# Selective-scan units of 32 channels by 4 states, with delta, du, B and C laid out by DMA

## The chip, the cores and the metric

One core of one Trainium2 chip runs the whole program: eight images go through two vision-Mamba layers in one launch. TensorE (PE), VectorE (DVE), ScalarE (ACT) and GpSimd (POOL) each work through their own instructions in order, and SyncE (SP) issues every DMA of this kernel. The metric is device time in microseconds of one execution. Data are float32, apart from a few bf16 tiles.

## The reference

Layer 0 maps each image of 64 by 64 tokens and 192 channels through a projection, a depthwise convolution, a two-directional SSD scan with 12 heads and 32 states, an output projection and an MLP. Layer 1 splits the channels in halves. One half goes through three convolutions; the other through layer norm, a projection to 192 channels, a depthwise convolution and a selective scan in four directions, after which the results are summed, normalised, gated and projected.

The change is in layer 1's selective scan:

```python
# per image and direction k: 192 channels, 16 states, L = 4096 tokens
x_dbl = jnp.einsum('bkdl,kcd->bkcl', xs4, x_proj_w)
dts, Bs, Cs = x_dbl[:, :, :6], x_dbl[:, :, 6:22], x_dbl[:, :, 22:]
delta = softplus(jnp.einsum('bkrl,kdr->bkdl', dts, dt_proj_w) + dt_proj_b)
A = -jnp.exp(A_logs)
def step(h, t):
    u_t, d_t, b_t, c_t = t
    h = jnp.exp(d_t[..., None] * A) * h + (d_t * u_t)[..., None] * b_t[:, :, None, :]
    return (h, jnp.einsum('bkdn,bkn->bkd', h, c_t))
```

So for every channel and state there is a recurrence along the tokens, h = dA * h + dB, with dA = exp(delta * A), dB = delta * u * B. Its results are multiplied by C and summed over the states. Here du stands for delta * u.

## The kernel before

**The scan's tiling.** `selective_scan` works in steps of LC = 1024 tokens: per image four steps forward (g = 0) and four backward (g = 1), each with two of the four directions. The 2 x 192 channels of a step are three tiles of 128 channels (t = 0, 2, 1; t = 2 holds the upper 64 channels of both directions). A unit of work is one [128, 1024] tile, whose partitions are 8 channels (UD) times 16 states (NS); a channel tile has 16 units (UN), and there are 8 x 8 x 3 x 16 = 3072 units in all.

**What a unit does.** For unit q:
- `fetch` (L1445) is a DMA that brings delta of its 8 channels from DRAM, each row repeated for 16 states, into a tile dA; it is issued 6 units ahead (AHEAD), into a ring of 7 tiles.
- `decay` (L1450) turns it into dA = exp(delta * A) on ScalarE, two units ahead and in place.
- `spread` (L1458) makes du repeated over the states in PSUM, by two matmuls of a 0/1 matrix with du in three bf16 terms that add up to the float32 value. Two PSUM tiles of two banks each are used in turn.
- `weigh` (L1473) multiplies that in PSUM by B, on VectorE.
- `scan` (L1480) is VectorE's recurrence h from dA, dB and the carry of the step before; behind it GpSimd multiplies h by C in place (L1482), all but the last column.
- `carry_on` (L1488, L1489) runs one unit later on ScalarE: it copies h's last column to the carry, and multiplies it by C.
- `gather` (L1500) runs every four units: TensorE sums four units' h over their states into a PSUM bank for each half of 512 tokens, ScalarE copies it to y (L1505), and `store` issues four DMAs (L1513).

**What feeds it.** `prepare` makes delta and du of the next channel tile: two matmuls, softplus on ScalarE, a product on GpSimd (L1409). Delta goes to DRAM (L1412); du is split into three bf16 terms by two casts on ScalarE (L1417, L1421) and two subtractions on GpSimd (L1419, L1423), goes to DRAM (L1426) and comes back as the matmuls' operand by twelve DMAs (L1434). `lay` (L1386) loads B and C, each row repeated for the 8 channels, as one tile each for a step and a direction.

**The order.** All instructions are pinned in the order in which the program writes them. The loop over q writes the scan's own pieces. In each half of a unit `Beside.half` adds pieces of the other work, as much as a credit allows: the next image's layer 0 (`conv0`, `ssd`, `mlp0`), and, for earlier images, `conv_branch`, `scan_outputs`, and the sums. So every engine's queue, SP's among them, mixes scan and other work in a fixed order. Those generators allocate their PSUM banks from a ring (`Shared.one`), of 4 banks while the scan runs; `gather` uses it too.

Of the kernel before, what the change touches and what calls it, by code (L numbers as in the profile page):

```python
# [17 lines left out]
L = HH * WW  # L18
PW = WW + 2
C = 192  # L20
# [19 lines left out]
UD = 128 // NS  # L40
UN = 128 // UD
# [34 lines left out]
class Shared:  # L76
# [5 lines left out]
    def __init__(self, tc):  # L82
        self.tc, self.nc, self.pin = tc, tc.nc, tc.keep_in_program_order
        self.k = {}
        self.singles = []
        self.side = None

# [22 lines left out]
def setup(cx, cp, dp, p0, p1):  # L110
# [141 lines left out]
    fold = cp.tile([128, UD], F32, tag="fold", name="fold")  # L252
    nc.vector.tensor_copy(fold, ident[:, 0:UD])
    for i in [32 * g + UD * v for g in range(4) for v in range(3)][1:]:
        nc.vector.tensor_add(fold, fold, ident[:, i : i + UD])
    for g in range(4):
        nc.vector.tensor_copy(
            k["spread"][32 * g : 32 * (g + 1), :].rearrange("p (n c) -> p n c", c=UD),
            bcast(fold[32 * g : 32 * (g + 1), 0:UD], 1, NS),
        )  # L260
    col = cp.tile([128, UD], F32, tag="col", name="col")
    nc.vector.tensor_copy(col, ident[:, 0:UD])
    for n in range(1, NS):
        nc.vector.tensor_add(col, col, ident[:, UD * n : UD * (n + 1)])
    k["gather"] = cp.tile([128, 32], F32, tag="gather", name="gather")
    nc.gpsimd.memset(k["gather"], 0.0)
    nc.vector.tensor_copy(k["gather"][:, 0:UD], col)
# [110 lines left out]
def conv0(cx, x):  # L378
# [3 lines left out]
    with cx.pool("cw0") as wp, cx.pool("v0", 2) as vp:  # L382
# [51 lines left out]
        def convolve(p, j):  # L434
            pss = [cx.one("ps_cv") for i in range(2)]
            yield from depthwise(cx, pss, [diag[0:64, j], diag[64:128, j]], pads[j])
            for i, ps in enumerate(pss):
                xc = xcs[p, 2 * j + i] = vp.tile([128, 512], F32, tag="xc", name="xc", bufs=7)
                pin(nc.scalar.activation(xc, ps, AF.Silu, bias=k["cb"][:, 2 * j + i : 2 * j + i + 1]))
            cx.exp_again()  # L440

        def turn(p, q):
# [26 lines left out]
            for rows, t in ((k["xrows"], xo), (k["prows"].rearrange("l k m -> l (k m)"), po)):  # L469
                at = p * R2 * WW  # L470
                dst = rows[at : at + R2 * WW].rearrange("(b q t) c -> q t b c", b=2, t=128)[q]
                pin(nc.sync.dma_start(out=dst, in_=t))
# [27 lines left out]
        for p in range(NP):  # L500
# [8 lines left out]
            for q in range(4):  # L509
                yield from turn(p, q)  # L510


def ssd(cx):
# [16 lines left out]
    with cx.pool("g0", 2) as gp, cx.pool("s0", 2) as sp:  # L530
# [72 lines left out]
        def decays(c):  # L603

            both = groups[c // GC][0]
            X = sp.tile([128, 2, NH, HP], F32, tag="X", name="X")
# [50 lines left out]
        def outputs(c):  # L657
# [19 lines left out]
            yield None  # L677
            psh = [cx.one("ps_h")[:, :INNER0] for d in range(2)]
# [7 lines left out]
            ps = pss[1].rearrange("p (h c) -> p h c", c=HP)  # L686
            pin(nc.vector.tensor_add(Hn, ps, Hn))
# [31 lines left out]
def mlp0(cx, x, x1):  # L719
# [9 lines left out]
    with cx.pool("mw0") as wp, cx.pool("m0", 2) as mp:  # L729
# [8 lines left out]
        def loads(i):  # L738
# [10 lines left out]
            def load_y(v, d):  # L749
                t = mp.tile([128, 2, INNER0], F32, tag=f"y{d}", name=f"y{d}", bufs=4 - 2 * d)  # L750
# [86 lines left out]
        def contract(i):  # L837
# [8 lines left out]
            pin(nc.sync.dma_start(out=x1[0:128, i * 2 * T : (i + 1) * 2 * T], in_=oa))  # L846
            for v, low in enumerate(lows):
                pin(nc.sync.dma_start(out=x1[128:C, (2 * i + v) * T : (2 * i + v + 1) * T], in_=ob[low]))
# [24 lines left out]
        for i in range(1, NI + 1):  # L873
# [7 lines left out]
            if i < NI:  # L881
                yield from project(i)


def conv_branch(cx, xl, short, out, side=None):

    nc, pin, k = cx.nc, cx.pin, cx.k
    with cx.pool("cw1") as wp, cx.pool("a1", 2) as ap:
# [49 lines left out]
        def second(r):  # L938
            ps = cx.one("ps_c2")[:CH]
            yield from conv(ps, pads[1][r % 2], ws[1])  # L940
            ys[r] = ap.tile([CH, 512], F32, tag="y", name="y")
# [331 lines left out]
class Beside:  # L1273
# [14 lines left out]
    def half(self):  # L1288

        self.cx.aside()  # L1290
# [13 lines left out]
    def finish(self):  # L1304

        for gen in self.stages:
            total = sum(cost or 0.0 for cost in gen)
# [4 lines left out]
def selective_scan(cx, us, ys, beside, images, start_image, tail):  # L1312
# [9 lines left out]
    AHEAD, BEHIND = 6, 2  # L1322
# [7 lines left out]
    units = [(n, i) for n in range(len(tiles)) for i in range(UN)]  # L1330
    U = len(units)
# [12 lines left out]
    with (  # L1344
# [4 lines left out]
        tc.tile_pool(name="ps1w", bufs=2, space=PSUM) as pw,  # L1349
    ):  # L1350
        u_of, rows_of, bc_of, delta_of, du_of, carries = {}, {}, {}, {}, {}, {}
        dAs, dBs, hs, late = {}, {}, {}, []
# [29 lines left out]
        def lay(m, e, i):  # L1382

            t = wp.tile([128, LC], F32, tag=f"bc{i}{e}", name=f"bc{i}{e}")
            at = NS * (2 * i + e)
            pin(nc.sync.dma_start(out=t, in_=repeated(rows_of[m][1][at : at + NS], True)))  # L1386
            bc_of.setdefault((m, e), []).append(t)

        def prepare(n):
# [8 lines left out]
            dl, du = (wp.tile([128, LC], F32, tag=v, name=v) for v in ("dl", "du"))  # L1398
# [10 lines left out]
            pin(nc.gpsimd.tensor_mul(du, dl, u_of[m][t]))  # L1409
            yield 6  # L1410
            dld = dp.tile([128, LC], F32, tag="dld", name="dld")
            pin(nc.sync.dma_start(out=dld, in_=dl))  # L1412
            delta_of[n] = dld
            yield 7

            terms = wp.tile([128, 3, LC], BF16, tag="terms", name="terms")
            pin(nc.scalar.copy(terms[:, 0, :], du))  # L1417
            yield 9
            pin(nc.gpsimd.tensor_sub(du, du, terms[:, 0, :]))  # L1419
            yield 11  # L1420
            pin(nc.scalar.copy(terms[:, 1, :], du))  # L1421
            yield 13
            pin(nc.gpsimd.tensor_sub(terms[:, 2, :], du, terms[:, 1, :]))  # L1423
            yield 17
            dud = dp.tile([3, 128, LC], BF16, tag="dud", name="dud")
            pin(nc.sync.dma_start(out=dud.rearrange("s p l -> p s l"), in_=terms))  # L1426
            yield 21

            dus = np_.tile([128, UN // 2, 512], BF16, tag="dus", name="dus")
            for half in range(2):  # L1430
# [7 lines left out]
                if half == 0:  # L1438
                    yield 23
# [299 lines left out]
```

## Time and profile before

| what | value |
|---|---|
| median of three runs | 16418.63 us (16416.5 to 16457.44) |
| span of the profiled execution | 16436.7 us |
| first scan starts, last scan starts | 902.0 us, 16192.7 us |
| mean granted TensorE clock | 0.827 |
| DMA | 3241.31 MB, 197 GB/s over the span; the queue's packets fill 78.5% of 16 engines |

DMA issues of the scan, all by SP:

| issue | count | KB each |
|---|---|---|
| dA<-dld (L1445) | 3072 | 512 |
| dud<-terms (L1426) | 192 | 768 |
| dus<-dud (L1434) | 2304 | 64 |
| bc<-bcd (L1386) | 256 | 512 |
| dld<-dl (L1412) | 192 | 512 |
| y<-y (L1513) | 3072 | 32 |

The longest waits of SP's own queue: 3764.0 us at L1445 for VectorE's scan (L1480) to free a tile of the ring, 474.6 us at L1445 for the DMA dA<-dld before it, 353.6 us at L607 (X<-xrows) for TensorE.

How to read it: a group's line has the code line, engine and operation, out<-in by the program's names, the shape, the count, then busy us and mean ns of one, then the engine's idle time just before that group and what ended most of it. The page's chain of waits is followed back from the last instruction, and its shares say on what the span was spent. Idle time of an engine that holds nothing up costs nothing.

### The profile page before, as it was taken

To read this page: it belongs to the slowest core of one execution; us is meant where nothing else is said; L and a number is where in the kernel's file an instruction comes from. 1 tells how busy PE (TensorE), PEld (TensorE's weight loads), DVE (VectorE), ACT (ScalarE), POOL (GpSimd) and SP (SyncE) were. 2 spreads that over 40 slices of the span, in tenths; PEclk is the share of its full clock that TensorE was granted. 3 is DMA by queue.
4 is the path that set the end of the run, shared out by engine and by line. 5 is a ranking of instruction groups with operands and counts; after the bars stand their busy time and mean duration, and the time that the engine had idled before them with its cause. 6 is when DMAs were issued, how large, how long until landed. Compare 5 with 4: busy or idle time off the path is not lost.

```text
span 16436.7 us, 210821 instructions
## 1 busy us (share of the span) xinstructions
PE 13372.1 (81%) x69608; PEld 4636.5 (28%) x69608; DVE 12230.0 (74%) x9264; ACT 10412.7 (63%) x20023; POOL 10527.5 (64%) x5766
## 2 busy tenths in 40 slices
PE   8977887788877897878888788777898788878876
PEld 4423322332223321333223332233322333211111
DVE  2178887886878767887678876788767886778994
ACT  4466677665775757757576575766657666655654
POOL 3158766775668656686567765677656775566773
PEclk9987888789887897878888798887988779877766
DMA  3288888788887888878888778887778877888885
GB/s 89 84 218 195 210 205 225 190 204 208 204 219 187 205 205 207 209 191 204 208 208 207 198 196 198 217 205 197 204 193 221 198 202 205 193 227 200 211 204 137
DMA packets 1602582, 3241.31 MB, mean 197 GB/s; under 512 B 390152, under 2 KB 841368, under 8 KB 1601496
## 3 DMA queue, kind: packets, MB, share of 16 engines
q1 hardware_dynamic: 1601496, 3227.83, 78.5%
q8 instruction: 559, 9.16, 0.3%
q14 instruction: 527, 4.32, 0.1%
HBM read 2548.91 MB, written 678.18 MB: 196 GB/s over the span
## 4 chain that ended last, share of the span: by engine, by line
PE 30%; DMA 16%; DVE 14%; ACT 13%; POOL 7%; issue 5%; SPq 2%; DVEq 0%; ACTq 0%; POOLq 0%
DVE h L1480 9%; DMA dA<-dld 5%; PE acc L1500 5%; DVE dB L1473 4%; PE ps_c L895 4%; PE ps_cv L343 3%; POOL h L1482 3%; ACT dA L1450 3%; PE dB L1458 2%; DMA dus<-dud 2%; PE ps_sum L1193 1%; ACT L107 1%; PE ps_m L799 1%; PE ps_y L696 1%; ACT h L830 1%
## 5 line engine op out<-in xcount | busy, mean ns | idle before, releaser
L1482 POOL TENSOR_TENSOR h<-h,bc 128x1023 f32<-128x1023 f32 x3072 | 7228.8, 2354 | 4585.2 <-DVE h L1480 3895.8
L1480 DVE TENSOR_TENSOR_SCAN h<-dA,carry,dB 128x1024 f32<-128x1024 f32 x3072 | 7200.8, 2344 | 820.7 <-ACT dA L1450 257.6
L1473 DVE TENSOR_TENSOR dB<-dB,bc 128x1024 f32<-128x1024 f32 x3072 | 3736.3, 1216 | 1827.5 <-PE dB L1458 1823.9
L1450 ACT ACTIVATE dA<-dA,neg_a 128x1024 f32<-128x1024 f32 x3072 | 3512.9, 1144 | 29.3 <-DMA dA<-dld 24.1
L1500 PE MATMUL acc<-h,gather 128*32 128x512 f32 x12288 | 2364.1, 730 | 596.5 <-ACT h L1489 329.0
L1458 PE MATMUL dB<-dus,spread 24*128 24x512 bf16 x6144 | 1370.2, 435 | 664.5 <-DVE h L1480 620.1
L1505 ACT COPY y<-acc 128x512 f32<-128x512 f32 x1536 | 884.8, 576 | 750.3 <-PE acc L1500 677.4
L895 PE MATMUL ps_c<-p,conv_w 96*96 96x512 f32 x2304 | 1287.7, 685 | 37.9 <-ACT p L915 26.9
L1488 ACT COPY carry<-h 128x1 f32<-128x1 f32 x3072 | 584.2, 190 | 856.9 <-DVE h L1480 854.4
L1458 PEld LDWEIGHTS <-spread 24*128 24x128 bf16 x6144 | 308.0, 93 | 2837.2 <-issue 1395.5
L1489 ACT ACTIVATE h<-h,bc 128x1 f32<-128x1 f32 x3072 | 905.2, 295 | 143.3 <-ACT carry L1488 1.8
L696 PE MATMUL ps_y<-X,M 64*64 64x64 f32 x12288 | 605.6, 270 | 418.6 <-issue 232.7
L624 ACT ACTIVATE M<-ps_d,ln_dt 128x64 f32<-128x64 f32 x3072 | 669.1, 335 | 314.6 <-PE ps_d L630 304.6
L343 PE MATMUL ps_cv<-pad,diag 64*64 64x512 f32 x6912 | 841.0, 605 | 7.1 <-ACT y L1505 5.1
L1500 PEld LDWEIGHTS acc<-h,gather 128*32 128x32 f32 x12288 | 311.2, 117 | 1636.3 <-issue 1040.1
L107 ACT ACT_TABLE_LOAD x577 | 740.3, 1283 | 10.0
L696 PEld LDWEIGHTS ps_y<-X,M 64*64 64x64 f32 x12288 | 548.8, 180 | 606.5 <-issue 275.5
L629 PE MATMUL ps_d<-R,after 128*128 128x384 f32 x1024 | 606.4, 685 | 31.2 <-ACT bc L618 14.6
L895 PEld LDWEIGHTS ps_c<-p,conv_w 96*96 96x96 f32 x2304 | 372.6, 180 | 785.5 <-issue 725.4
L618 ACT COPY bc<-ps_t 64x256 f32<-64x256 f32 x256 | 93.4, 365 | 716.7 <-PE ps_t L613 716.5
L373 PE MATMUL ps_h<-oa,w1a 128*128 128x256 f32 x1536 | 484.0, 438 | 76.6 <-ACT y L1505 32.2
L1370 PE MATMUL ps_xp<-u,xp 128*108 128x512 f32 x768 | 470.0, 699 | 92.5 <-DMA u<-u 76.0
(243 smaller groups left out, 18412.4 us busy)
## 6 DMA issues: line engine op xcount, KB each, us to landing
dA<-dld SPq DMA_DIRECT2D x3072, 512.0 KB
dud<-terms SPq DMA_DIRECT2D x192, 768.0 KB
dus<-dud SPq DMA_DIRECT2D x2304, 64.0 KB
bc<-bcd SPq DMA_DIRECT2D x256, 512.0 KB
y<-yrows SPq DMA_DIRECT2D x256, 384.0 KB
u<-u SPq DMA_DIRECT2D x192, 512.0 KB
dld<-dl SPq DMA_DIRECT2D x192, 512.0 KB
y<-y SPq DMA_DIRECT2D x3072, 32.0 KB
```

Source lines behind the costliest of these rows:

```text
L107: self.pin(self.nc.scalar.preload_act_table_set("natural_log_exp_and_others"))
L343: pin(nc.tensor.matmul(ps[64 * b : 64 * (b + 1)].rearrange("p (h w) -> p h w", w=WW), lhsT=diag[:, t, :], rhs=pad[64 * i : 64 * (i + 1), b ...
L696: pin(nc.tensor.matmul(psy[d][here, h * HP : (h + 1) * HP], lhsT=M[here, d, h, :], rhs=X[here, d, h, :], start=True, stop=True,))
L895: pin(nc.tensor.matmul(ps.rearrange("p (h w) -> p h w", w=WW), lhsT=w[:, t, :], rhs=pad[:, dy : dy + RB, dx : dx + WW], start=t == 0, stop ...
L1450: pin(nc.scalar.activation(dAs[q], dAs[q], AF.Exp, scale=k["neg_a"][:, steps[m][1], t, i : i + 1]))
L1458: pin(nc.tensor.matmul(dBs[q][:, half, :], lhsT=k["spread"][at : at + 3 * UD, :], rhs=du_of[n][at : at + 3 * UD, i // 2, :], start=True, s ...
L1473: pin(nc.vector.tensor_mul(dBs[q], dBs[q], of(q)[0]))
L1480: pin(nc.vector.tensor_tensor_scan(order(h, g), order(dA, g), order(dB, g), carry, ALU.mult, ALU.add))
L1482: pin(nc.gpsimd.tensor_mul(h[:, rest], h[:, rest], C_[:, rest]))
L1489: pin(nc.scalar.activation(end, end, AF.Identity, scale=C_[:, last : last + 1]))
L1500: pin(nc.tensor.matmul(ps[32 * v : 32 * (v + 1)], lhsT=k["gather"], rhs=hs[q - 3 + v][:, here], start=True, stop=True))
L1505: pin(nc.scalar.copy(y[:, here], ps))
```

## The change

A unit becomes 32 channels times 4 states (UD = 32, NU = 4). There are still 16 units to a channel tile and 3072 in all. Eight units are a group (GROUP): two blocks of 32 channels, in turn, through four groups of states.

- `fetch` now brings delta (dlr) and du (dur), each row repeated for 4 states; one tile of each serves the four units of a block. They are loaded a group ahead, in rings of four.
- `decay` reads dlr and writes dA in a ring of three.
- `spread`, its constant, the bf16 terms and dus are gone. du is made in place of u, stored as float32, and read back by `fetch`.
- `lay` loads one tile of B and one of C for every 4 states, four of each for a direction, each row repeated for 32 channels. They are issued from the scan's loop two units behind the last use of the tile that they replace.
- `weigh` multiplies B and dur, both in SBUF, into one PSUM tile of two banks. It is written right behind the scan of the unit before.
- GpSimd's product covers all 1024 columns and goes from h to a tile of its own, g (ring of four; h has a ring of three). `carry_on` comes two units later and only copies, and only where another step follows.
- `gather` runs every two units and accumulates over the four groups of states in a PSUM bank of its own, whose partitions are two halves of tokens times two blocks. So there is one y of [128, 512] in eight units, which two DMAs store.
- `Shared.later` holds a store back for some halves of a unit (y 5, xrows and prows 3, x1 2).
- Rings: xc 7 to 6, X 2 to 3, the forward y of `mlp0` 4 to 3, y of `conv_branch` to 1; the PSUM ring has 5 banks while the scan runs. In `ssd` the add to Hn stands ahead of the matmuls ps_h. In the first half of a unit `Beside.half` comes ahead of `prepare`, in the second half behind it.

```diff
-UD = 128 // NS
-UN = 128 // UD
+UD = 32
+NU = 128 // UD
+UN = 128 // UD * (NS // NU)
...
+    def later(self, halves, call):
+        self.waiting.append([halves, call])
+    def half(self):
+        for item in self.waiting:
+            item[0] -= 1
+        self.flush(0)
+    def flush(self, least=None):
+        while self.waiting and (least is None or self.waiting[0][0] <= least):
+            self.waiting.pop(0)[1]()
...
-        def lay(m, e, i):
-            t = wp.tile([128, LC], F32, tag=f"bc{i}{e}", name=f"bc{i}{e}")
-            at = NS * (2 * i + e)
-            pin(nc.sync.dma_start(out=t, in_=repeated(rows_of[m][1][at : at + NS], True)))
+        def lay(m, e, state):
+            at = NS * e + NU * state
+            for i, v in enumerate("BC"):
+                t = np_.tile([128, LC], F32, tag=v, name=v, bufs=NS // NU)
+                pin(nc.sync.dma_start(out=t, in_=repeated(rows_of[m][1][2 * NS * i + at : 2 * NS * i + at + NU], True)))
...
-            pin(nc.gpsimd.tensor_mul(du, dl, u_of[m][t]))
+            pin(nc.gpsimd.tensor_mul(du, dl, du))
...
+            pin(nc.sync.dma_start(out=dud, in_=du))
...
+        def fetch(q, which):
+            n, _, _, cg, _ = of(q)
+            tag = ("dl", "du")[which]
+            t = np_.tile([128, LC], F32, tag=tag + "r", name=tag + "r", bufs=4)
+            pin(nc.sync.dma_start(out=t, in_=repeated(delta_of[n][which][UD * cg : UD * (cg + 1)], False)))
...
+            dAs[q] = np_.tile([128, LC], F32, tag="dA", name="dA", bufs=3)
...
+        def weigh(q):
+            n, _, _, cg, _ = of(q)
+            dBs[q] = pw.tile([128, LC], F32, tag="w", name="dB")
+            pin(nc.vector.tensor_mul(dBs[q], bc(q, "B"), reps[n, cg, 1]))
+        def scan(q):
+            carry, g, _ = carry_of(q)
+            dA, dB = dAs.pop(q), dBs.pop(q)
+            h = hs[q] = np_.tile([128, LC], F32, tag="h", name="h", bufs=3)
+            pin(nc.vector.tensor_tensor_scan(order(h, g), order(dA, g), order(dB, g), carry, ALU.mult, ALU.add))
+            gs[q] = np_.tile([128, LC], F32, tag="g", name="g", bufs=4)
+            pin(nc.gpsimd.tensor_mul(gs[q], h, bc(q, "C")))
...
+        def gather(q):
+            n, m, t, cg, state = of(q)
+            image, g, s = steps[m]
+            if state == 0:
+                late.append(py.tile([128, 512], F32, tag="acc", name="acc"))
+            ps = late[-1]
+            for half in range(2):
+                for b in range(2):
+                    at = 64 * half + UD * b
+                    pin(nc.tensor.matmul(
+                        ps[at : at + UD], lhsT=k["gather"], rhs=gs[q - 1 + b][:, halves[half]],
+                        start=state == 0, stop=state == NS // NU - 1,
+                    ))
...
+                if q % 2 == 1 and q > 2:
+                    _, m0, t0, cg, state = of(q - 2)
+                    if t0 == 2 and cg == 1:
+                        lay(m0, 1, state)
+                    if t0 == 1 and cg == 3 and m0 + 1 < len(steps):
+                        lay(m0 + 1, 0, state)
...
+                ahead = q - q % GROUP + GROUP
+                if q % GROUP < 4 and ahead < U:
+                    fetch(ahead + q % 2, q % GROUP // 2)
...
                     if half == 0:
-                        if q > 0:
-                            carry_on(q - 1)
-                        if q + 1 < U:
-                            spread(q + 1)
-                        scan(q)
+                        if q > 1:
+                            carry_on(q - 2)
+                        scan(q)
+                        if q + 1 < U:
+                            weigh(q + 1)
                     elif q + 2 < U:
                         decay(q + 2)
```

## The prediction

> **What bounds the kernel now.** I read the page's totals first, then the chain of waits, the costliest groups, the stretches by stage, the waits, and a piece of the timeline.
>
> ```profile
> span 16436.7 us, 210821 instructions
> PE 13372.1 (81%) x69608; PEld 4636.5 (28%) x69608; DVE 12230.0 (74%) x9264; ACT 10412.7 (63%) x20023; POOL 10527.5 (64%) x5766
> PE 30%; DMA 16%; DVE 14%; ACT 13%; POOL 7%; issue 5%; SPq 2%; DVEq 0%; ACTq 0%; POOLq 0%
> ```
>
> No engine is full, and the chain changes hands all the time: engines that run in order wait for each other. So the question is which of these waits end, not how much work.
>
> ```profile
> L1482 POOL TENSOR_TENSOR h<-h,bc 128x1023 f32<-128x1023 f32 x3072 | 7228.8, 2354 | 4585.2 <-DVE h L1480 3895.8
> L1480 DVE TENSOR_TENSOR_SCAN h<-dA,carry,dB 128x1024 f32<-128x1024 f32 x3072 | 7200.8, 2344 | 820.7 <-ACT dA L1450 257.6
> L1473 DVE TENSOR_TENSOR dB<-dB,bc 128x1024 f32<-128x1024 f32 x3072 | 3736.3, 1216 | 1827.5 <-PE dB L1458 1823.9
> L1458 PE MATMUL dB<-dus,spread 24*128 24x512 bf16 x6144 | 1370.2, 435 | 664.5 <-DVE h L1480 620.1
> L1505 ACT COPY y<-acc 128x512 f32<-128x512 f32 x1536 | 884.8, 576 | 750.3 <-PE acc L1500 677.4
> L1488 ACT COPY carry<-h 128x1 f32<-128x1 f32 x3072 | 584.2, 190 | 856.9 <-DVE h L1480 854.4
> L1489 ACT ACTIVATE h<-h,bc 128x1 f32<-128x1 f32 x3072 | 905.2, 295 | 143.3 <-ACT carry L1488 1.8
> ```
>
> The largest wait of VectorE is in front of L1473: 1824 us until TensorE's spread (L1458) is there. That matmul is short (two of 435 ns a unit) but stands in TensorE's order behind conv and MLP matmuls.
>
> ```profile
> 889.00:16193.00 15304.00, 12457.13 (x63672) 4239.01 (x63672) 12015.65 (x8776) 9973.65 (x19078) 10265.27 (x5500) 0.82 0.82 205
> 6600.00:6900.00 300.00, 254.92 (x1868) 98.11 (x1864) 255.37 (x148) 233.54 (x440) 208.17 (x105) 0.92 0.88 223
> 6900.00:7400.00 500.00, 382.69 (x3128) 166.51 (x3128) 411.52 (x424) 283.38 (x756) 405.20 (x267) 0.74 0.76 187
> 7400.00:7800.00 400.00, 337.78 (x1513) 142.13 (x1514) 304.36 (x216) 297.29 (x488) 245.41 (x111) 0.90 0.82 204
> 7800.00:8300.00 500.00, 445.81 (x1214) 120.05 (x1212) 338.37 (x222) 293.40 (x503) 286.58 (x150) 0.86 0.79 200
> ```
>
> Columns: stretch, length, busy PE, PEld, DVE, ACT, POOL, clock, DMA share, GB/s. Scanning fills 15304 us, or 4.98 us for each of 3072 units; 889 + 244 = 1133 us lie outside. The four stages are layer 0's convolution, its SSD, its MLP, and layer 1's conv branch. VectorE leads in the first two (85% and 82%), TensorE in the last two (84% and 89%), DMA is at 0.76 to 0.88 in all.
>
> ```profile
> 15701.28 2.35 DVE L1480 TENSOR_TENSOR_SCAN h<-dA,carry,dB 128x1024 f32<-128x1024 f32 x1
> 15703.55 1.21 DVE L1473 TENSOR_TENSOR dB<-dB,bc 128x1024 f32<-128x1024 f32 x1
> 15703.77 2.35 POOL L1482 TENSOR_TENSOR h<-h,bc 128x1023 f32<-128x1023 f32 x1 [1.24 <-DVE h L1480]
> 15704.89 2.35 DVE L1480 TENSOR_TENSOR_SCAN h<-dA,carry,dB 128x1024 f32<-128x1024 f32 x1
> ```
>
> Where little else is in the way a unit takes 3.61 us (15704.89 - 15701.28), all of it VectorE's. GpSimd's product starts with VectorE's next product: the end of a scan sets off both.
>
> **The change, part by part.** Sums are against the execution of 16436.7 us; the median of the runs, 16418.6, is 18 us less.
>
> *Spread removed.* TensorE loses 6144 matmuls, 1370 us, and VectorE's wait of 1824 us has no object any more; TensorE's own waits for a free dB (1125 us before the loads, 620 us before the matmuls) go too. The gain lies between 0 (the next wait is as late) and 1824 us. Late next is ScalarE's decay, which stands behind evictions of the other layers' matmuls, so that TensorE still holds VectorE, but at two units' distance instead of one. By stage the spread costs TensorE 0.446 us a unit: 73, 85, 79 and 89 scans give 33, 38, 35 and 40 us, which bring it to 74, 69, 76 and 81%, while VectorE stays at 85, 82, 76 and 68%. The first two stages thus have little to win, the last two more. I take half: -912 us.
>
> *dB from two SBUF tiles.* Same size, same engine: 3072 x 1216 ns stays. The one row with two SBUF inputs, a 128x384 product at setup (L179), took 557 ns against 536 to 540 ns for those with a PSUM tile, so alone it costs next to nothing more (20 ns x 3072 = 61 us at most; taken as 0). What no row shows is such a product beside GpSimd: every VectorE product in the scan now has a PSUM operand. Bounds: 0, and a whole GpSimd product each time, 2354 ns x 3072 = 7231 us. In favour of the low end: GpSimd's product is as long as the scan (2354 and 2344 ns) and, if it starts behind the new product, is over when the scan is. Only GpSimd's other work can then stand in the way, 10265 - 7229 - 817 = 2219 us in 15304, 14.5% of the time, with some 0.6 us left of an operation of about 1.2 us: 0.09 us a unit. I take 0.15 us, since a product pushed back can hinder the next one: 461 us.
>
> The Trainium skill (SBUF — State Buffer, Who interferes with whom) speaks against the change here: a VectorE instruction with two SBUF inputs and a GpSimd instruction that reads SBUF exclude each other, and whichever comes second is blocked for the whole of the first. No row of this trace shows it. By that rule the sum depends on who is first after each scan: near mine if VectorE is, near the high bound if GpSimd is.
>
> *ScalarE.* Scaling the last column (L1489) goes, 905 us; the carry copy stays in 2304 of 3072 units (438 us for 584) and looks back two units, not one, so that its 854 us of waiting shrink; 384 y copies replace 1536 (221 us for 885); the two casts go (400 us). ScalarE falls by 2115 us, from 65% of the scan to 51%. It was not full, so I count nothing beyond the half above.
>
> *GpSimd.* Two subtractions per tile go (817 us); the product has one column more (2 ns). Also nothing beyond.
>
> *DMA.* Per unit dA's 512 KB becomes two such tiles per four units: 1611 MB to 805. The 2304 spread loads (151 MB) go, dud shrinks by 50 MB, B and C grow from 256 to 1024 tiles (134 to 537 MB): 604 MB less of 3228. SP issues 5376 fewer (8704 to 3328) and no longer waits in every unit for the scan to free dA (3764 us). But 128 of the 384 groups of eight units now carry eight B/C tiles and four fetches, 6.3 MB, beside 3.1 MB of other traffic: 46 us at the mean 205 GB/s, 39 us at the 242 GB/s of the fastest 100 us that I saw, against 40 us for eight units. Bounds 0 and 128 x 6 = 770 us; I take 0, as fetches are a group ahead and B and C four units, and leave it to the half given back. Each C load waits on SP for a GpSimd product two units back; behind it stand X and y loads of the other layers, which then start late.
>
> *Shorter rings, later stores, the Hn add moved up.* h falls from 7 buffers to 3 (plus 4 for the products): a scan needs the product three units back, 15 us for 2.4 us of work. xc 7 to 6 is covered by TensorE's order (its last readers come before the next writers). y 4 to 3 and the one-deep y of the conv branch are covered by loads a turn ahead; GpSimd's product of the first waits 153 us for its load now, ScalarE's write of the second 157 us for TensorE; both could double. Later stores take waits such as 156 us (SP for oa) and 108 us (for xo) off SP's order, on which nothing ends directly. The Hn add waits 230 us for GpSimd now; earlier, a whole product before each would be 256 x 2.35 = 603 us. All 0; cover gone, up to 0.9 ms together.
>
> Sum: 16437 - 912 + 461 = 15986; less 18 for the median: **15970 us**, own range 15300 to 16400.
>
> **Rivals.**
> *A, slower: GpSimd holds the product back.* Place: right behind each scan, where both start within 0.2 us. If a product meets GpSimd at any time of its work, 67% of the scan, and waits half an operation of 2354 ns, that is 0.79 us a unit, 2422 us. VectorE: 12016 busy + 2422 + (3288 - 1824) other idle + 1133 outside = 17035, or 17020. It decides from 912/3072 = 0.30 us a unit on. For it: the same start, and SSD, where GpSimd has 405 of 500 us: less 23 for the subtractions, plus 85 products of 1.22 us = 104, it is 486 us if nothing overlaps. Against: the lengths match, so the two can take turns. Chance 0.31. Its extreme, waiting out every product, gives 16437 - 912 + 7231 = 22760 us, a few per cent of that.
> *B, the wait only moves.* Decay, B/C bursts or the short rings are late exactly where the spread was. Nothing gained, with the 461 us of hindrance or without: 16420 to 16880, centre 16600. For it: DMA at 0.82 and TensorE at 81%. Against: 604 MB less. Chance 0.13.
> *C, everything is won.* 1824 us with no hindrance: 14600 to 15200. For it: 3.61 us units exist. Against: the two stages in which VectorE is already at 82 to 85%. Chance 0.10.
>
> **Numbers.** Forecast 0.46, A 0.31, B 0.13, C 0.10. Under 0.3% (49 us) a measurement cannot tell. Faster: C and nearly all of the forecast: 0.55. Same: 0.06, from the forecast's edge and B's. Slower: 0.39, from A and most of B. Range 15100 to 17100: it holds the forecast, B and the middle of A.
>
> **What would show it.** Right: L1473's successor idles little and lasts 1.2 to 1.4 us; spans on GpSimd stay near 2.35 us; VectorE is above 76% of the span. A shows as a product or a GpSimd row stretched towards 3.5 us. B shows as VectorE's idle time in front of the scan, released by dA or by B and C loads. I am wrong above all if the two engines' products cannot take turns.

## The result and the profile after

| | before | after |
|---|---|---|
| median | 16428.15 us (16416.5 to 16457.44, 4 runs) | 19802.73 us (19794.14 to 19859.58, 4 runs) |
| profiled execution's span | 16436.7 us | 19799.7 us |

The change made the kernel slower: the ratio is 1.205, 95% interval 1.203 to 1.207. The forecast was 15970 us, its range ended at 17100 us.

From the page of the changed kernel: the span, busy time by engine, the mean busy share of the 16 DMA engines in tenths over 40 slices, the DMA queue (packets, MB, share of 16 engines), the chain of waits by engine, and four groups of instructions.

```profile
span 19799.7 us, 184227 instructions
PE 13204.0 (67%) x63464; PEld 4572.6 (23%) x63464; DVE 13616.2 (69%) x9235; ACT 8490.1 (43%) x14634; POOL 12227.8 (62%) x5381
...
DMA  3234433444434444444444444444444444443333
...
q1 hardware_dynamic: 1257432, 2623.55, 40.7%
...
DVE 4%; DMA 3%; PE 1%; SPq 1%; ACT 1%; issue 0%; POOL 0%; DVEq 0%; ACTq 0%; POOLq 0%
...
L1482 POOL TENSOR_TENSOR g<-h,C 128x1024 f32<-128x1024 f32 x3072 | 9524.3, 3102 | 5431.1 <-DVE h L1480 4101.0
L1480 DVE TENSOR_TENSOR_SCAN h<-dA,carry,dB 128x1024 f32<-128x1024 f32 x3072 | 7194.5, 2342 | 3488.4 <-ACT carry L1490 1979.8
L1473 DVE TENSOR_TENSOR dB<-B,dur 128x1024 f32<-128x1024 f32 x3072 | 4979.0, 1621 | 844.1 <-DMA B<-bcd 389.9
...
L1395 PE MATMUL ps_xp<-u,xp 128*108 128x512 f32 x768 | 556.3, 836 | 1180.7 <-DMA u<-u 1178.8
```

Three things stand here. No engine is fuller than 69% although everything takes longer. The DMA engines, at 78.5% before, look idle at 40.7%, with 604 MB less to move. And yet several lines wait for a load: TensorE 1179 us for u at L1395, which was 76 us before (there the line is L1370). The wait that the change was to remove, 1824 us ahead of L1473, is down to 844, but the one ahead of the scan grew from 821 to 3488. The chain breaks off after a tenth of the span here, so it says little.

That line of TensorE before:

```profile
L1370 PE MATMUL ps_xp<-u,xp 128*108 128x512 f32 x768 | 470.0, 699 | 92.5 <-DMA u<-u 76.0
```

A low share and late loads fit together if few of the 16 engines have all the work. This is the DMA view of the changed kernel in the window from 9068 to 9100 us, in 40 slices of 0.8 us: the engines' mean busy share in tenths, and GB/s.

```profile
DMA  8699962222232222269622223843522222222222
GB/s 342 172 317 245 236 136 86 102 108 102 102 123 102 102 108 102 98 174 375 220 86 102 108 102 128 323 142 129 164 108 102 102 102 102 87 92 102 102 102 102
```

For most of the time the share is pinned at 2 tenths, which is near 4 of 16 engines, and the rate at 102 to 108 GB/s, mostly 102, or some 26 GB/s for each of four. In between other transfers reach 317 to 375 GB/s. So 512 KB over four engines take some 5.1 us (524288 bytes at 102 GB/s). The trace's DMA packets, counted over the whole span, say the same: four or five are in flight at once for 61% of it (before: 1.5%), and at least four for 91%. Before, the most frequent number was sixteen, for 32% of the span. What SP's own queue does meanwhile, from the timeline (start, duration, engine, line, operation):

```profile
9066.55 0.57 SPq L1412 DMA_DIRECT2D B<-bcd  x1
...
9068.88 5.60 SPq L1412 DMA_DIRECT2D B<-bcd  x1
9074.58 4.84 SPq L1412 DMA_DIRECT2D C<-bcd  x1
...
9082.38 5.03 SPq L857 DMA_DIRECT2D x<-oa  x1
```

An issue takes 0.57 us at first, and then about 5 us, the length of one such load, as it would if each had to wait until a load ahead of it is done. SP issues in order, so whatever stands behind it is late too, even a transfer of another stage (L857 stores layer 0's output).

The waits of the changed kernel (engine, tile, line, what it waited for: us in total, times, longest):

```profile
DVE h L1480 <- ACT carry L1490: 1979.8, 279, 38.9
...
PEld ps_xp L1395 <- DMA u<-u: 1281.7, 125, 35.8
...
DVE h L1480 <- ACT dA L1455: 1004.3, 138, 26.6
...
ACT po L472 <- DMA prows<-po: 612.0, 40, 45.2
```

These are few and long: 279 waits for the carry make 1980 us, 7.1 us each. ScalarE's carry is a copy of 0.19 us, but in ScalarE's order it stands behind evictions that wait for TensorE or for a transfer. So VectorE's idle time would largely be a late transfer seen through other engines; in experiment 1, with the loads on time, the wait for the carry falls to 453 us.

The second cost is in the durations. The scan lasts what it did (2342 ns), but dB's product has a mean of 1621 ns for 1216, and GpSimd's product 3102 for 2354. From the timeline of the changed kernel, near its end, where little else runs:

```profile
19470.79 1.23 DVE L1473 TENSOR_TENSOR dB<-B,dur 128x1024 f32<-128x1024 f32 x1
...
19470.90 3.32 POOL L1482 TENSOR_TENSOR g<-h,C 128x1024 f32<-128x1024 f32 x1 [0.41 <-DVE h L1480]
19472.15 2.35 DVE L1480 TENSOR_TENSOR_SCAN h<-dA,carry,dB 128x1024 f32<-128x1024 f32 x1
...
19478.39 2.35 POOL L1482 TENSOR_TENSOR g<-h,C 128x1024 f32<-128x1024 f32 x1 [0.43 <-DVE h L1480]
19479.49 2.33 DVE L1473 TENSOR_TENSOR dB<-B,dur 128x1024 f32<-128x1024 f32 x1 [1.25 <-DMA B<-bcd]
```

In the first unit VectorE starts 0.11 us ahead: its product takes 1.23 us and GpSimd's 3.32, 0.97 more than alone. Two units later a late B tile lets GpSimd start first: it takes 2.35 us, and VectorE's product 2.33 instead of 1.23. Whichever comes second stands still, and the profile counts that as its busy time.

So there are two suspects, and they can be undone separately. Theory D: the repeated loads run on 4 engines, since their source's outermost step is 4 long. Theory L: VectorE's product of two SBUF tiles and GpSimd's work shut each other out.

### The profile page after: what moved, and what is told of

Its sections match the earlier page's. It is cut to its first block, busy times and chain, and to the rows that moved or that the text cites. A ratio compares the mean times of both kernels' runs of the same rounds, so it can differ in the third digit from the quotient of the medians.

```text
span 19799.7 us, 184227 instructions
## 1 busy us (share of the span) xinstructions
PE 13204.0 (67%) x63464; PEld 4572.6 (23%) x63464; DVE 13616.2 (69%) x9235; ACT 8490.1 (43%) x14634; POOL 12227.8 (62%) x5381
## 3 DMA queue, kind: packets, MB, share of 16 engines
q1 hardware_dynamic: 1257432, 2623.55, 40.7%
## 5 line engine op out<-in xcount | busy, mean ns | idle before, releaser
L1482 POOL TENSOR_TENSOR g<-h,C 128x1024 f32<-128x1024 f32 x3072 | 9524.3, 3102 | 5431.1 <-DVE h L1480 4101.0
L1480 DVE TENSOR_TENSOR_SCAN h<-dA,carry,dB 128x1024 f32<-128x1024 f32 x3072 | 7194.5, 2342 | 3488.4 <-ACT carry L1490 1979.8
L1473 DVE TENSOR_TENSOR dB<-B,dur 128x1024 f32<-128x1024 f32 x3072 | 4979.0, 1621 | 844.1 <-DMA B<-bcd 389.9
L1502 PE MATMUL acc<-g,gather 128*32 128x512 f32 x12288 | 2984.9, 770 | 2064.3 <-POOL g L1482 1758.4
L1455 ACT ACTIVATE dA<-dlr,neg_a 128x1024 f32<-128x1024 f32 x3072 | 3512.0, 1155 | 1903.3 <-DVE h L1480 1647.1
L1395 PE MATMUL ps_xp<-u,xp 128*108 128x512 f32 x768 | 556.3, 836 | 1180.7 <-DMA u<-u 1178.8
L1502 PEld LDWEIGHTS acc<-g,gather 128*32 128x32 f32 x12288 | 373.9, 120 | 4060.3 <-POOL g L1482 2913.9
L674 PE MATMUL ps_s<-xw,both 64*32 64x384 f32 x2048 | 310.3, 656 | 498.3 <-POOL xw L659 464.5
L768 POOL TENSOR_TENSOR y<-y,y 128x768 f32<-128x768 f32 x128 | 256.7, 2013 | 532.7 <-DMA y<-yrows 502.5
L659 POOL TENSOR_TENSOR xw<-X,toend 128x768 f32<-128x768 f32 x256 | 381.6, 1491 | 288.6 <-DMA X<-xrows 259.4
L465 PE MATMUL ps_p<-xp,xc 64*128 64x140 f32 x3072 | 289.8, 324 | 399.3 <-ACT po L472 394.0
L1435 POOL TENSOR_TENSOR u<-dl,u 128x1024 f32<-128x1024 f32 x192 | 471.4, 2455 | 112.8 <-DMA bcd<-rows 82.0
```

The costliest lines, as they stand in the source:

```text
L1395: pin(nc.tensor.matmul(ps[:NXP], lhsT=k["xp"][:, g, t, :], rhs=u_of[m][t][:, here], start=t == 0, stop=t == 2))
L1455: pin(nc.scalar.activation(dAs[q], reps[n, cg, 0], AF.Exp, scale=k["neg_a"][:, steps[m][1], t, i : i + 1]))
L1473: pin(nc.vector.tensor_mul(dBs[q], bc(q, "B"), reps[n, cg, 1]))
L1480: pin(nc.vector.tensor_tensor_scan(order(h, g), order(dA, g), order(dB, g), carry, ALU.mult, ALU.add))
L1482: pin(nc.gpsimd.tensor_mul(gs[q], h, bc(q, "C")))
L1502: pin(nc.tensor.matmul(ps[at : at + UD], lhsT=k["gather"], rhs=gs[q - 1 + b][:, halves[half]], start=state == 0, stop=state == NS // NU - 1,))
```

## The experiments

Ratios are to the kernel before, which ran on the same chip each time (medians 16431.1, 16434.1 and 16432.3 us in the three sets).

**1. Turned.** In the changed kernel's repeated loads the outermost step of the source runs over 4: the 4 states of B and C, or the 4 repeats of delta and du. Here a channel's 4 states lie side by side, so the outermost step is 32. Bytes, tiles and instructions are the same.

```diff
-    nc.vector.tensor_copy(k["gather"], ident[:, 0:UD])
+    nc.vector.tensor_copy(k["gather"], ident[:, 0:128:NU])
...
-                pin(nc.sync.dma_start(out=t, in_=repeated(rows_of[m][1][2 * NS * i + at : 2 * NS * i + at + NU], True)))
+                pin(nc.sync.dma_start(out=t, in_=repeated(rows_of[m][1][2 * NS * i + at : 2 * NS * i + at + NU], False)))
...
-            pin(nc.sync.dma_start(out=t, in_=repeated(delta_of[n][which][UD * cg : UD * (cg + 1)], False)))
+            pin(nc.sync.dma_start(out=t, in_=repeated(delta_of[n][which][UD * cg : UD * (cg + 1)], True)))
...
-    d["a_logs"] = a.transpose(0, 1, 5, 3, 2, 4).reshape(2, 3, 128, UN)
+    d["a_logs"] = a.transpose(0, 1, 3, 5, 2, 4).reshape(2, 3, 128, UN)
```

> The changed kernel with the partitions turned: channel times 4 plus state, not state times 32 plus channel, so that the outermost step of every repeated load (dlr, dur, B, C) has 32 entries and not 4; the same bytes, issues and instructions. Theory D (a repeated load with an outermost step of 4 runs on 4 of the 16 DMA engines, at some 102 to 108 GB/s, 4.8 us for 512 KB, and SP's queue fills): the DMA share in bursts is no longer 0.22, SP's issues of 512 KB fall from up to 5 us to 0.5, time 15900 to 16900 us. Theory L (VectorE's product with two SBUF operands and GpSimd's product hinder each other, and that is the loss): nothing changes, 19300 us or more.

Measured: 16357.7 us, ratio 0.995 (0.993 to 0.997). Against the changed kernel that is 3445 us less, inside theory D's range. From its page:

```profile
span 16363.6 us, 184227 instructions
...
PE 12867.4 (79%) x63464; PEld 4473.6 (27%) x63464; DVE 13799.6 (84%) x9235; ACT 8491.2 (52%) x14634; POOL 12481.1 (76%) x5381
...
q1 hardware_dynamic: 1288152, 2623.68, 49.6%
...
L1482 POOL TENSOR_TENSOR g<-h,C 128x1024 f32<-128x1024 f32 x3072 | 9751.6, 3176 | 2718.3 <-DVE h L1480 2127.3
L1480 DVE TENSOR_TENSOR_SCAN h<-dA,carry,dB 128x1024 f32<-128x1024 f32 x3072 | 7196.5, 2343 | 971.2 <-ACT carry L1490 452.8
L1473 DVE TENSOR_TENSOR dB<-B,dur 128x1024 f32<-128x1024 f32 x3072 | 5170.4, 1683 | 207.0 <-DMA dur<-dud 101.7
```

The same 2624 MB; four or five packets are in flight for only 2% of the span, and the wait ahead of the scan is 971 us instead of 3488. Both products are still stretched, and VectorE is at 84%: with the loads on time it is the bound.

**2 and 3. One operand.** The product of the changed kernel, and of the turned one, takes one SBUF tile and a column of B; B's other columns are left out of the result.

```diff
-            pin(nc.vector.tensor_mul(dBs[q], bc(q, "B"), reps[n, cg, 1]))
+            pin(nc.vector.tensor_scalar_mul(dBs[q], reps[n, cg, 1], bc(q, "B")[:, 0:1]))
```

> The changed kernel with the product dB made from one SBUF tile: dur times the first column of B as a scalar for each partition (B's other columns are left out of the computation; all loads stay). Theory L: the product stays at 1.23 us (mean now 1.62), GpSimd's at 2.35 us (mean now 3.10), time 16000 to 17000 us. Theory D: the rows get short as well, but the 4-engine loads still bound it: 18700 to 19600 us.

> Both: partitions turned and dB from one SBUF tile (B's other columns left out of the computation). What is left is the change without either cost. Theory D plus a smaller L: 14900 to 15900 us, 400 to 1200 us below the run with turned partitions alone. Theory L alone: the same as the run with one operand.

Measured: 19508.0 us (ratio 1.187, 1.184 to 1.190) in the changed kernel, 15375.5 us (0.936, 0.934 to 0.939) in the turned one. Products of the latter, from its page's groups:

```profile
L1482 POOL TENSOR_TENSOR g<-h,C 128x1024 f32<-128x1024 f32 x3072 | 7232.2, 2355 | 4662.6 <-DVE h L1480 3672.1
...
L1473 DVE TENSOR_SCALAR dB<-dur,B 128x1024 f32<-128x1024 f32 x3072 | 3954.2, 1287 | 209.7 <-DMA dur<-dud 101.1
```

GpSimd is back at 2355 ns, and VectorE's product takes 1286 to 1290 ns, never more. So theory L is right, and its price depends on the loads: 982 us where they are on time (16358 - 15376), 295 us in the changed kernel (19803 - 19508), where VectorE waits for loads anyway. As the single-operand form is 54 ns longer than the undisturbed product (1233 ns, 166 us in all), 982 is rather a lower figure. Experiment 3 is also the change without either cost: 1056 us less than before. It changes the operation along with the operand; experiment 10 moves an operand and keeps the operation.

**4. The kernel before, turned.** The outermost step of its repeated loads is 16, and sixteen packets in flight is what its trace shows most. With a channel's 16 states side by side, delta's loads have one of 8. Nothing of the change is in this kernel.

```diff
-            pin(nc.sync.dma_start(out=dAs[q], in_=repeated(delta_of[n][UD * i : UD * (i + 1)], False)))
+            pin(nc.sync.dma_start(out=dAs[q], in_=repeated(delta_of[n][UD * i : UD * (i + 1)], True)))
```

(B and C, the constants and A's layout are turned to match.)

> The kernel before with its partitions turned the other way: channel times 16 plus state, so that the outermost step of dA's load has 8 entries and not 16, and that of B and C 8 and not 16; the same bytes and instructions, with constants to match. Theory D: those loads run on 8 engines; 1745 MB on 8 engines at 27 GB/s each is 8.1 ms, beside some 8.9 ms of each engine's other packets, so the first 8 engines are full at 17000 us: 17000 to 19000 us. Theory L, or any theory in which the order of the repeated loads does not matter: 16400 us, the same as before.

Measured: 18202.8 us, ratio 1.108 (1.105 to 1.111). Its queue and the chain of waits, from its page:

```profile
q1 hardware_dynamic: 1574872, 3227.72, 60.3%
...
DMA 37%; PE 26%; DVE 13%; ACT 9%; POOL 7%; issue 4%; SPq 3%; DVEq 0%; POOLq 0%; ACTq 0%
DMA dA<-dld 16%; DVE h L1480 8%; DVE dB L1473 4%; PE ps_cv L343 4%; PE acc L1500 3%; DMA X<-xrows 3%; DMA u<-u 3%; POOL h L1482 2%; DMA dus<-dud 2%; PE ps_c L895 2%; ACT dA L1450 2%; DMA prows<-po 2%; DMA part<-y 2%; PE dB L1458 2%; DMA xa<-in_x_dram 2%
```

The same line of the kernel before:

```profile
DVE h L1480 9%; DMA dA<-dld 5%; PE acc L1500 5%; DVE dB L1473 4%; PE ps_c L895 4%; PE ps_cv L343 3%; POOL h L1482 3%; ACT dA L1450 3%; PE dB L1458 2%; DMA dus<-dud 2%; PE ps_sum L1193 1%; ACT L107 1%; PE ps_m L799 1%; PE ps_y L696 1%; ACT h L830 1%
```

DMA's share of the chain rises from 16% to 37%, dA's loads from 5% to 16%, while the queue's busy share falls from 78.5% to 60.3%. Eight packets are in flight for 43% of the span, against 4.5% before. Order alone costs 1772 us here. That says that the order counts, and theory D's range held it, but in both kernels partitions and outermost step were changed together. The next one separates them.

**5. Split loads.** The changed kernel with its own partition order; each repeated load is four DMAs of 32 partitions, whose outermost step is 32.

```diff
-                pin(nc.sync.dma_start(out=t, in_=repeated(rows_of[m][1][2 * NS * i + at : 2 * NS * i + at + NU], True)))
+                for v4 in range(NU):
+                    row = rows_of[m][1][2 * NS * i + at + v4 : 2 * NS * i + at + v4 + 1]
+                    src = bass.AP(row.tensor, row.offset, [[0, UD], list(row.ap[1])])
+                    pin(nc.sync.dma_start(out=t[UD * v4 : UD * (v4 + 1)], in_=src))
...
-            pin(nc.sync.dma_start(out=t, in_=repeated(delta_of[n][which][UD * cg : UD * (cg + 1)], False)))
+            for v4 in range(NU):
+                pin(nc.sync.dma_start(out=t[UD * v4 : UD * (v4 + 1)], in_=delta_of[n][which][UD * cg : UD * (cg + 1)]))
```

> The changed kernel with its own order of partitions, and each repeated load (dlr, dur, B, C) issued as four DMAs of 32 partitions, so that each has an outermost step of 32; the same bytes, 10240 issues in place of 2560. Theory D (the outermost step of 4 is what counts, not the order of the partitions): 16300 to 17000 us, near the run with turned partitions, a little more for SP's 7680 extra issues of some 0.3 us. If the order of the partitions in itself made the difference: 19000 us or more.

Measured: 16497.6 us, ratio 1.003 (1.002 to 1.004). The same tiles, partitions and bytes, with four times as many issues of these loads (10240 for 2560), take 3305 us less. Sixteen packets in flight is the most frequent number again (22% of the span; four or five: 1.7%). The outermost step is the cause, not the order of partitions. That settles theory D.

**6 to 8. How the engines shut each other out.** The turned kernel's product lasts 1232 to 1233 ns in most cases, but up to 10.0 us, and its mean is 450 ns longer than the median. From its timeline in a stretch of SSD:

```profile
9011.32 2.34 DVE L1480 TENSOR_TENSOR_SCAN h<-dA,carry,dB 128x1024 f32<-128x1024 f32 x1
...
9012.51 1.46 POOL L659 TENSOR_TENSOR xw<-X,toend 128x768 f32<-128x768 f32 x1
9013.70 6.39 DVE L1473 TENSOR_TENSOR dB<-B,dur 128x1024 f32<-128x1024 f32 x1
9013.94 0.38 POOL L560 TENSOR_TENSOR dt<-raw,dtb 128x96 f32<-128x96 f32 x1
...
9014.29 1.46 POOL L608 TENSOR_TENSOR R<-upto,da 128x768 f32<-128x768 f32 x1
9015.72 0.98 POOL L670 TENSOR_TENSOR M<-M,skip 128x384 f32<-128x384 f32 x1
9016.67 2.33 POOL L1482 TENSOR_TENSOR g<-h,C 128x1024 f32<-128x1024 f32 x1
```

VectorE's product is issued during `xw` and ends at 9020.09, 1.09 us after GpSimd's fifth instruction in a row (9016.67 + 2.33 = 9019.00). It gets in at none of the four ends between. Two theories: GpSimd keeps VectorE out while it has work queued (K), or the two take turns by instruction (R). One kernel cuts GpSimd's product into halves; another puts a GpSimd write of two columns ahead of it and of five SSD products, an instruction that reads nothing. A third of the same set asks what the later stores bring.

```diff
-            pin(nc.gpsimd.tensor_mul(gs[q], h, bc(q, "C")))
+            for here in halves:
+                pin(nc.gpsimd.tensor_mul(gs[q][:, here], h[:, here], bc(q, "C")[:, here]))
```
```diff
+            pin(nc.gpsimd.memset(k["spread"][:, 0:2], 0.0))
             pin(nc.gpsimd.tensor_mul(gs[q], h, bc(q, "C")))
```

> The changed kernel with its partitions turned, and GpSimd's product g in two halves of 512 columns. With partitions turned alone: 16358 us, VectorE's product 1683 ns on average, 1233 ns at the median, up to 10 us where GpSimd has several instructions in a row. Theory R (the two engines take turns by instruction, in the order in which they ask): waits get shorter, the mean falls below 1550 ns, time 15900 to 16250 us. Theory K (GpSimd keeps VectorE out until it has nothing left to run): the second half follows the first at once, nothing is won, and 0.2 us of GpSimd's fixed time is added to each unit: 16350 to 16900 us.

> The changed kernel with its partitions turned, and a GpSimd memset of two columns of an unused tile (it writes and reads nothing) ahead of every product g and of the five GpSimd operations of each SSD chunk. Theory K: a gap without a read lets VectorE in; its product's mean falls from 1683 to below 1450 ns, the longest from 10 us to below 4 us, time 15700 to 16200 us. Theory R, or a memset that keeps the hold: the mean stays, and some 4350 memsets of 0.1 us or more make it 16400 to 16900 us.

Measured: halves 16495.6 us (1.004, 1.002 to 1.005) with a product of 1769 ns on average, longest 10.3 us; short writes 16512.2 us (1.005, 1.003 to 1.006) with 1758 ns, longest 10.2 us. Both are worse than the turned kernel. Halving GpSimd's product does not shorten the wait, so taking turns by instruction (R) is not the rule. But the expectation that a write without a read would open a gap was wrong, and K is no strict rule either. In the whole trace of the turned kernel 590 products are stretched by over 0.3 us, and each ends about 1.1 us after the end of a GpSimd instruction. 370 waited through one instruction; in 365 of these GpSimd's next one stood ready, and yet VectorE got in ahead of it. The other 220 waited through two to six; in 214 of these GpSimd had nothing ready when VectorE got in. What decides this at the end of an instruction is left open.

**9. Stores at once.** `Shared.later` of the turned kernel calls the store directly.

```diff
-        self.waiting.append([halves, call])
+        call()
```

> The changed kernel with its partitions turned, and every store issued at its place in the program instead of some halves later (y, xrows and prows, x1). The prediction priced the later stores at 0: 16300 to 16420 us. If SP's order is on the path, as its 1084 us of waits at one store line and the full queue in the changed kernel suggest, it is slower: 16500 to 17000 us.

Measured: 16386.2 us, ratio 0.997 (0.995 to 0.998), against 0.993 to 0.997 with later stores: the intervals overlap. The two are some 30 us apart, which these runs don't tell from nothing.

**10. du from PSUM.** If two SBUF operands are the trouble, one of them should come from PSUM again. In the turned kernel TensorE spreads a block's du, once for its four units, into a PSUM tile; dB goes to SBUF. du's loads are gone.

```diff
+        def spread(q):
+            n, _, _, cg, _ = of(q)
+            t = reps[n, cg, 1] = pw.tile([128, LC], F32, tag=f"w{cg % 2}", name="dus")
+            for here in halves:
+                pin(nc.tensor.matmul(t[:, here], lhsT=k["spread"][:, cg, :], rhs=delta_of[n][1][:, here], start=True, stop=True))
...
-            dBs[q] = pw.tile([128, LC], F32, tag="w", name="dB")
+            dBs[q] = np_.tile([128, LC], F32, tag="dB", name="dB")
...
-    cx.singles = [ctx.enter_context(tc.tile_pool(name="ps", bufs=5, space=PSUM))]
+    cx.singles = [ctx.enter_context(tc.tile_pool(name="ps", bufs=3, space=PSUM))]
```

> The turned kernel (a channel's 4 states side by side), in which du reaches VectorE's product from PSUM: TensorE spreads the 32 channels of a block over 4 states by two float32 matmuls with a 0/1 matrix, once for a block's four units (768 spreads, 1536 matmuls), into one PSUM tile of two banks for each of the two blocks; dB goes to SBUF; du's repeated loads (768) and its way through DRAM are gone; the other work's PSUM ring has 3 banks instead of 5. Theory (two SBUF operands of VectorE and GpSimd's work shut each other out): the product has a PSUM operand again, as before the change, so its longest instance falls from 10.0 us to under 1.5 us and GpSimd's product to about 2.36 us; the time is near that of the turned kernel with one operand, 15376 us, or up to half of the new matmuls' 1284 us (1536 at 836 ns, the float32 row L1395) above it: 15300 to 16000. Rival (TensorE takes over): 12867 + 1284 = 14151 us of matmuls are 92% of 15376 us and a ring of 3 banks makes the other work wait, so VectorE waits for the spread or the decay again: 16100 to 16600 although the products are short. If the lock has nothing to do with the operand's place, the product's longest instance stays above 5 us.

Measured: 18137.8 us, ratio 1.104 (1.102 to 1.106). Neither the theory's time nor the rival's. The product's and the scan's instances (min/median/max in ns), and a piece of the timeline:

```profile
L1481 DVE TENSOR_TENSOR dB<-B,dus x3072: 1183/1190/1223, 885.4 to 17882.3; 128x1024 f32<-128x1024 f32 x192
```
```profile
L1488 DVE TENSOR_TENSOR_SCAN h<-dA,carry,dB x3072: 2331/3072/8141, 899.7 to 17883.6; 128x1024 f32<-128x1024 f32 x192
```
```profile
8996.01 2.33 POOL L1490 TENSOR_TENSOR g<-h,C 128x1024 f32<-128x1024 f32 x1
...
8996.22 4.27 DVE L1488 TENSOR_TENSOR_SCAN h<-dA,carry,dB 128x1024 f32<-128x1024 f32 x1
...
8998.31 3.25 POOL L973 TENSOR_TENSOR o<-o,sh 96x512 f32<-96x512 f32 x1
```

The product is undisturbed, as theory L said: never over 1.223 us. But the scan now has dA and dB both in SBUF, and it is the scan that waits: it starts 0.21 us behind GpSimd's product, which ends at 8998.34, and ends itself at 9000.49, 2.15 us later. GpSimd's next instruction (L973, 1.26 us at the median) starts at 8998.31, then stands still in its turn and takes 3.25. On average the scan is 3123 ns instead of 2342, some 2400 us in all. The expectation had moved the second operand from one instruction to another and priced only the first. It is the clearest proof of theory L, as the wait went where the two SBUF operands went. Against experiment 3 the kernel loses 2762 us (18138 - 15376); how much of that is the scan's and how much the ring's of three banks and the spread's was not separated. The spread was also priced too low: the trace has two records for each of its 1536 matmuls, and they keep TensorE busy for 1929 us, not 1284.

## Why the prediction was wrong, step by step

**The step that failed is "DMA".** It counted bytes ("604 MB less of 3228"), reckoned bursts at the mean 205 and the fastest 242 GB/s of the trace, gave "Bounds 0 and 770 us" and took 0. Measured: 3445 us lost (19803 - 16358), over four times the upper bound. The rate of the whole queue was taken for the rate of each transfer. All of the old kernel's repeated loads had an outermost step of 16, so no row of its trace showed one on four engines; but the arguments of `repeated` give the outermost step, 4 where it was 16. The old trace did have narrower transfers: where only its 1 KB packets were in flight, nine in ten of them of the dus loads with 8 partitions, there were eight or nine at once for 61% of the time. At 102 GB/s, 2560 loads of 5.1 us (768 each of delta and du, 512 each of B and C) make 13.1 ms of work on four engines. An estimate of the rest: 40.7% of 19800 us is 8059 us a DMA engine on average, less 13.1/4 ms is 4780 us of other packets; if those are spread evenly, the four engines have 17.9 of 19.8 ms. The count of packets gives the same: at least four in flight for 91% of the span. So four engines are nearly full, at a mean share that looks idle.

The Trainium skill (DMA: Bandwidth & Descriptors, Why a DMA increments its semaphore by 16 and not by 1) has this rule: the number of engines is the largest one up to 16 that divides the slowest dimension, longer than 1, of both access patterns. With fewer than 16, on a queue such as SP's, they are the lowest-numbered ones. Loads of this kind would then not spread over different fours. The share of 2 tenths at 102 GB/s and experiments 1, 4 and 5 agree with it; which engines they were, the traces don't show. The prediction did not use it.

**"SP issues 5376 fewer and no longer waits"**: the count was right, the conclusion not. SP's issues of the four repeated loads took 1.1 to 2.0 us on average and up to 11.5, against 0.6 and at most 2.5 in the turned kernel, and the X, y and u loads behind them came late, as the same paragraph had feared of C loads; it had left that "to the half given back".

**"Spread removed", -912 us**: near. Experiment 3, with neither cost, gains 1056 us, and VectorE's idle time ahead of L1473 is 210 us there instead of 1828. But the 1056 holds all other parts of the change too, so it doesn't show the spread's share by itself; that half of 1824 us came so close is partly luck.

**"dB from two SBUF tiles", +461 us**: the mechanism was right, its size off by two. Measured 982 us, 0.32 us a unit for 0.15. Right was that VectorE is first behind most scans (its median is 1233 ns, its undisturbed length), so that GpSimd pays, 0.97 us, off the path. Wrong was the reckoning of GpSimd's other work as "some 0.6 us left of an operation": VectorE waited through up to six operations in a row (five in the case shown, whose product took 6.39 us). In the turned kernel 590 of 3072 products (19%, against the 14.5% reckoned) are stretched by over 0.3 us, and by 2.3 us on average, not 0.6. The Trainium skill (SBUF — State Buffer, Who interferes with whom) said that the second is blocked for the whole of the first; the turned kernel's trace shows it blocked longer than that in 220 of 590 cases.

**Rival A** had this mechanism at 0.79 us a unit, "decides from 0.30 us a unit on". At 0.32 it should just have decided; the turned kernel is 0.5% faster than before. The difference is the gain, 1056 for 912, which puts the point at 0.34. Its sign, a GpSimd row stretched towards 3.5 us (3102 ns on average in the changed kernel), came without its price. **Rival B** named "B/C bursts" among the waits that could take the spread's place, and its sign (VectorE idle ahead of the scan, released by dA and late loads) is what the profile shows, but at a price of nothing gained, not of 3.4 ms lost. **Rival C** would have been near (15375 against 14600 to 15200) had both costs been absent.

**Later stores, priced 0**: some 30 us, not told from nothing (experiment 9). ScalarE and GpSimd's lesser work, the shorter rings and the Hn add were not tried by themselves; what they gained or lost is inside experiment 3's 1056 us.

The corrected sum, in one order of undoing: 16431 - 1056 + 982 + 3445 = 19802. It comes out by construction, as its terms are differences of these runs. The order counts: with the loads late, the two operands cost only 295 us.

## What to carry to other kernels

When a DMA's access pattern changes, write out its outermost step on both sides before counting bytes: here a pattern that begins with 4 was a transfer at a quarter of the engines, and a zero step in front (a repeat) counted like any other. Put the long dimension outermost, or split the load; reordering partitions by channel made the same change 0.5% faster than before instead of 20% slower. And before two operands of a VectorE instruction move to SBUF beside a busy GpSimd, count GpSimd's longest row of instructions, not its average share, and look at every VectorE instruction whose operands move, the scan included.

## What the runs showed of the hardware

- A DMA share of 0.2 with late loads was work queued on four engines. Each of them moved some 26 GB/s in rows of 4 KB (a packet takes 162 ns at the median). Before, the average was 197 GB/s at 78.5% of 16 engines, 15.7 GB/s for each that worked, and a packet of 4 KB took 256 ns.
- The cost reached transfers that the change left alone, behind the repeated loads in SP's order: 1282 us (98 before) of waits of TensorE's weight loads for u, 612 us (157 before) of ScalarE's for a store of layer 0.
- VectorE's wait for GpSimd is not the length of one instruction. It lasted through up to six GpSimd instructions (10.0 us), and was shortened neither by halving GpSimd's product (10.3 us at most) nor by short writes in between (10.2 us).
- The wait is inside the instruction's own span, so a stretched row (1683 ns on average beside a median of 1233), and not an idle time, is what tells of it.
